# A four-layer graph network on one core: the launch's tests become a last sample of the schedule, the preparation moves among the first steps, and the order is searched anew

## The chip, the cores and the metric

The kernel runs on one core of one Trainium2 chip. A core has five engines, each with its own stream of instructions executed in order: TensorE (PE, with weight loads listed apart as PEld), VectorE (DVE), ScalarE (ACT), GpSimd (POOL) and SyncE (SP), which here only issues DMAs. The metric is the device time of one execution in microseconds (us), lower is better.

## The reference

The input `x` has 32 samples of 512 nodes with 256 features in float32, and one adjacency matrix of 512 by 512. Four layers follow one another, each with a normalisation ahead of it and its result added to `x`:

```python
h = jnp.maximum(_layernorm(x, axis=-1), 0.0); x = x + L0(h, adj, ...)  # 4-head attention, masked, output projection
h = jnp.maximum(_layernorm(x, axis=-1), 0.0); x = x + L1(h, adj, ...)  # MLP, graph attention (no mask), MLP, graph attention (mask)
h = jnp.maximum(_layernorm(x, axis=-1), 0.0); x = x + L2(h, adj, ...)  # 4-head graph attention, masked
h = jnp.maximum(_layernorm(x, axis=-1), 0.0); x = x + L3(h, adj, adj[None], ...)  # 8-head graph attention, mask and prior
```

In layer 0 `scores = q k^T / 8` where `adj != 0`, softmax, times `v`, times `wo`. In the graph attentions the score of nodes i and j is `leaky_relu(f1[i] + f2[j])`, followed by a softmax over j. Layer 3 adds `softplus(beta) * log(adj + 1e-6)` to the scores.

## The kernel before

Everything of the weights and masks stays in the on-chip memory; samples pass through one by one. A tile of nodes is 128 rows, so a sample is 4 such tiles (`NT`), and a 128 by 512 float32 square is one "block" (57 buffers) on chip or one "bank" (8) of the accumulator memory.

**Preparation** (lines 423 to 601, one block of code with an order written by hand). SP, ScalarE and GpSimd issue the loads of the adjacency (lines 430 and 431) and of all weights (432 to 463). VectorE casts the adjacency, TensorE transposes it (494 to 496), ScalarE copies it (500, 501). Masks are made from it: `mask0T` (546), `mask1` and `mask1T` (598 to 601, on GpSimd), and `mask3T`, which is the Relu, then Ln (510), then Exp scaled by `beta` (544). `projections` (483) multiplies the attention vectors of layers 2 and 3 into extra columns of `w2` and `w3`. The bias columns are turned by 12 small matmuls (566), the output bias `boa` and the column-sum correction `b2a` come from more matmuls (587 to 596).

**Tests.** Layers 0, 2 and 3 leave out the usual subtraction of a maximum in their softmax. Whether that is safe is tested on the weights: grams of `wq` and `wk` (517 to 535), row maxima of the adjacency (537), squares of the projected columns (553 to 559), and a short reduction (571 to 582), which ends in one integer, `go`. At the end of the kernel function all engines read `go` into a register (line 1367) and branch to `pipelined` (the quick form, taken with these inputs) or `general` (a safe loop).

**The schedule.** `pipelined` writes each sample's four layers as steps into a `Plan` (line 70), 32 samples in all. `Plan.order` (line 156) then decides the order in which all steps are emitted: a greedy simulation of the five engines with costs from `cost` (line 311). At each turn it takes the step that could start first; among equals the one with the smallest due time, `step.due = s * self.period - step.tail - step.urgent` (line 169), where `tail` is the longest chain behind the step and `urgent` comes from the table `URGENT` (line 47). `STARTS`, `PACE` and `LAYERS` (lines 44 and 45) say from when on a sample's layer may start; a step's sample may be at most `AHEAD = 3` samples ahead of the oldest one in flight. `issue` (line 265) emits the steps; the last 16 pieces of preparation, the list `late` (lines 619 and 620: products for `W_fc` and `W_hand`, and the final product for `mask3T`), are emitted one at every second step behind step 100. Since every recorded step is emitted by one line, nearly all instructions of the samples carry line 275 in the profile and are told apart by the names of their tiles: `h`, `pt`, `mm`, `sc`, `p`, `av`, `total`, `sm`.

Each layer opens with `norm_t` (line 648): statistics on VectorE, the inverse root `rs` on GpSimd, the scaled `h` on ScalarE, transposes `pt` on TensorE. Layer 0 (733) goes on with q, k and v, eight pairs of score matmuls `sc`, exponentials `p` on ScalarE, mask products and sums `total` on VectorE, and `av`. `normalise` (708) divides by the sums with the help of small DMAs. `separable` (902) serves layers 2 and 3; for the last samples it sums on TensorE (`direct`, 926).

Of the kernel before, what the change touches and what calls it, by code (L numbers as in the profile page):

```python
# [20 lines left out]
P = 128  # L21
# [21 lines left out]
PERIOD = 57.0  # L43
STARTS, PACE = (0.0, 11.0, 54.0, 70.0), 29.0
LAYERS = (0.0, 55.0, 178.0, 198.0)

URGENT = {
    "h:0": 49, "pt:0": 23, "mm:0": 7, "sc:0": 89, "p0:0": -655, "total:0": -158, "av:0": -3, "rc:0": -39,
    "oT:0": -103, "stats:1": 94, "h:1": 11, "pt:1": 6, "hT:1": 93, "mm:1": -5, "r1:1": -511, "total:1": -50,
    "rs1:1": -41, "av:1": -24, "o2:1": -243, "fb:1": -11, "s:1": 20, "r2:1": 94, "pt:2": 134, "mm:2": -7,  # L50
    "p3:2": -20, "av:2": -185, "total:2": -319, "sm:2": -35, "ue:2": -200, "stats:3": 6, "ms:3": -69,
    "h:3": -156, "hT:3": 112, "mm:3": -58, "e8:3": -19, "p3:3": -989, "av:3": -489, "total:3": -598,
    "raw:3": -11,
}
BLOCKS, KEEP = 57, 2
KEEP_BANKS = 0

LATE = 100
# [11 lines left out]
class Plan:  # L70
# [85 lines left out]
    def order(self):  # L156
# [16 lines left out]
        free = {tag: [0.0] * bufs for tag, (bufs, _) in self.tags.items()}  # L173
        held = {}
# [170 lines left out]
def gnn_stack_kernel(ctx: ExitStack, tc: tile.TileContext, a: dict, out: bass.AP):  # L345
# [21 lines left out]
    def load_rows(name, eng, cols):  # L367

        src = a[name]
        k = src.shape[0] // P  # L370
        t = const.tile([P, k, cols], F32, name=name)
        eng.dma_start(t[:, :, : src.shape[1]], T(src, "(k p) c -> p k c", p=P))
        return t
# [5 lines left out]

    def load_bcast(pool, name, eng, n):  # L380
        t = pool.tile([P, n], F32, name=name)
        load(t, name, eng)
        return t
# [30 lines left out]

# [5 lines left out]
    afc = first.tile([P, 2 * HID], F32, name="afc")  # L420
    ahd = first.tile([P, 2 * D], F32, name="ahd")
    prf = first.tile([P, HID], BF16, name="prf")
# [3 lines left out]
    with prep_stack, tc.manual_schedule():  # L426
# [5 lines left out]
        nc.scalar.dma_start(w2[:, :, H2 : H2 + D], T(a["L2_W"], "(k p) c -> p k c", p=P))  # L432
        src = a["L2_a"]
        a2 = prep.tile([P, 2, F2], F32, name="a2")
        nc.scalar.dma_start(a2, bass.AP(tensor=src.tensor, offset=src.offset, ap=[[0, P], [1, 2 * F2]]))
        for k in range(KD):
            nc.gpsimd.dma_start(
                T(w3[:, k, H3 : H3 + D], "p (h f) -> p h f", h=H3), T(a["L3_W"][:, k * P : (k + 1) * P, :], "h p f -> p h f")
            )
        bt = load_bcast(prep, "beta", nc.scalar, 1)  # L440
# [8 lines left out]
        wq = load_rows("wqT", nc.scalar, D)  # L449
        wk = load_rows("wkT", nc.sync, D)  # L450
        s3 = load_bcast(prep, "L3_a_src", nc.sync, D)
        d3 = load_bcast(prep, "L3_a_dst", nc.sync, D)
        m2 = load_rows("mlp2_w", nc.sync, D)
        wo = load_rows("woT", nc.sync, D)
        bo = load_bcast(prep, "bo", nc.sync, D)
        wv = load_rows("wvT", nc.sync, D)
        m1 = load_rows("mlp1_w", nc.sync, HID)
        wfc = load_rows("W_fc", nc.sync, HID + 2)
        f1a, r1a = wfc[:, :, HID : HID + 1], wfc[:, :, HID + 1 :]
        load(afc, "a_fc", nc.sync)  # L460
        wh = load_rows("W_hand", nc.sync, D + 2)
        load(ahd, "a_hand", nc.sync)
        w3o = load_rows("L3_WoT", nc.sync, D)

# [4 lines left out]
        one = prep.tile([P, 1], F32, name="one")  # L469
        nc.vector.memset(one, 1.0)  # L470
        H = H2 + H3
        tests = prep.tile([P, 2 * H + 5], F32, name="tests")
        nc.vector.memset(tests, 0.0)


        def project(w, kn, heads, f, vec, dst):

            for k in range(kn):
                pr = prep.tile([P, heads, f], F32, name="pr")
                nc.vector.tensor_tensor(pr, T(w(k), "p (h f) -> p h f", h=heads), vec, op=ALU.mult)  # L480
                nc.vector.tensor_reduce(dst(k), pr, axis=AX.X, op=ALU.add)

        def projections(w, h, f, vs, vd):
            project(lambda k: w[:, k, h : h + D], KD, h, f, vs, lambda k: w[:, k, :h])
            project(lambda k: w[:, k, h : h + D], KD, h, f, vd, lambda k: w[:, k, 3 * h + D :])
            nc.vector.tensor_scalar(w[:, :, h + D : 2 * h + D], w[:, :, :h], ALPHA - 1.0, None, op0=ALU.mult)
            nc.vector.tensor_scalar(w[:, :, 2 * h + D : 3 * h + D], w[:, :, 3 * h + D :], ALPHA, None, op0=ALU.mult)


        top = prep.tile([P, NT], F32, name="top")  # L490
# [6 lines left out]
        at = [prep.tile([P, N], F32, name="at", bufs=NT) for _ in range(NT)]  # L497
        m3 = [mask3T[:, j, :] for j in range(NT)]
        for j in range(NT):
            nc.scalar.copy(at[j], adjT[j])  # L500
            nc.scalar.activation(m3[j], adjT[j], AF.Relu)
        projections(w2, H2, F2, a2[:, 0:1, :].to_broadcast([P, H2, F2]), a2[:, 1:2, :].to_broadcast([P, H2, F2]))

        ab = prep.tile([P, 1], F32, name="ab")
        nc.vector.tensor_scalar(ab, bt, -1.0, None, op0=ALU.mult)
        nc.vector.tensor_tensor(ab, ab, bt, op=ALU.max)
        nc.scalar.activation(ab, ab, AF.Exp, scale=-1.0)
        nc.scalar.activation(ab, ab, AF.Ln, bias=one)
        for j in range(NT):
            nc.scalar.activation(m3[j], m3[j], AF.Ln, bias=eps)  # L510
        projections(w3, H3, F3, T(s3, "p (h f) -> p h f", h=H3), T(d3, "p (h f) -> p h f", h=H3))
        nc.vector.scalar_tensor_tensor(beta, bt, 0.0, ab, op0=ALU.max, op1=ALU.add)

        grams = []
        for w, name in ((wq, "bq"), (wk, "bk")):
            gp = pp.tile([64, N], F32, name="gp", bufs=2)
            for h in range(4):  # L520
                c = slice(h * 64, (h + 1) * 64)
                r = row[:, spans[name] + h * 64 : spans[name] + (h + 1) * 64]
                for k in range(KD):
                    nc.tensor.matmul(gp[:, c], w[:, k, c], w[:, k, c], start=(k == 0), stop=False)
                nc.tensor.matmul(gp[:, c], r, r, start=False, stop=True)
            gram = prep.tile([64, D], F32, name="gram", bufs=2)
            nc.vector.tensor_copy(gram, gp[:, :D])
            grams.append(gram)
        gp = pp.tile([64, N], F32, name="gp", bufs=2)
        for n in range(2):  # L530
            for h in range(4):
                c = slice(h * 64, (h + 1) * 64)
                nc.tensor.matmul(
                    gp[:, n * D + h * 64 : n * D + h * 64 + 64], grams[n][:, c], grams[1 - n][:, c], start=True, stop=True
                )
        for t in range(NT):
            nc.vector.tensor_reduce(top[:, t : t + 1], adjf[:, t, :], axis=AX.X, op=ALU.max)

        ok = prep.tile([P, NT], F32, name="ok")
        nc.vector.tensor_scalar(ok, top, 0.0, None, op0=ALU.is_gt)  # L540
        nc.vector.tensor_scalar(top, top, 0.0, None, op0=ALU.max)
        nc.scalar.activation(top, top, AF.Ln, bias=eps)
        for j in range(NT):
            nc.scalar.activation(m3[j], m3[j], AF.Exp, scale=beta)
        for j in range(NT):
            nc.vector.tensor_scalar(mask0T[:, j, :], at[j], 0.0, None, op0=ALU.not_equal)
        gab = prep.tile([64, D], F32, name="gab")
        nc.vector.tensor_copy(gab, gp[:, :D])
        nc.vector.tensor_tensor(gab, gab, gp[:, D:], op=ALU.mult)
        nc.vector.tensor_reduce(  # L550
            tests[:64, 2 * H + 1 : 2 * H + 5], T(gab, "p (h f) -> p h f", h=4), axis=AX.X, op=ALU.add
        )
        sq = prep.tile([P, KD, 2 * H], F32, name="sq")
        o = 0
        for w, h in ((w2, H2), (w3, H3)):
            for v in (w[:, :, :h], w[:, :, 3 * h + D :]):
                nc.vector.tensor_tensor(sq[:, :, o : o + h], v, v, op=ALU.mult)
                o += h
        nc.vector.tensor_tensor(tests[:, : 2 * H], sq[:, 0, :], sq[:, 1, :], op=ALU.add)
        bad = prep.tile([P, NT], F32, name="bad")  # L560
        nc.vector.tensor_scalar(bad, top, beta, SAFE_PRIOR, op0=ALU.mult, op1=ALU.is_le)
        nc.vector.tensor_tensor(bad, bad, ok, op=ALU.mult)
        nc.vector.tensor_reduce(tests[:, 2 * H : 2 * H + 1], bad, axis=AX.X, op=ALU.add)
        cp = pp.tile([P, N], F32, name="tp")
        for c in range(12):
# [446 lines left out]
    def general(stack):  # L1012

        for f in late:
            f()
# [409 lines left out]
```

## Time and profile before

| quantity | value |
|---|---|
| runs of the kernel, median (lowest to highest) | 4020.88 us (4020.18 to 4025.28), 3 runs |
| profiled execution, its own time | 4023.19 us |
| span of the profiled execution (first to last instruction) | 4021.3 us |
| TensorE, busy | 3933.0 us, 98% |
| VectorE, busy | 3303.2 us, 82% |
| ScalarE, busy | 2992.8 us, 74% |
| GpSimd, busy | 659.0 us, 16% |
| DMA | 274.80 MB, mean 68 GB/s |
| chain that ended last | 60% TensorE, 17% VectorE, 5% ScalarE, 4% DMA |

The profile is one execution recorded by the hardware. "Busy" is the time in which an engine had at least one instruction in work; matmuls overlap, so a busy TensorE is not one at its peak. A row of the timeline gives the start, the length, the engine, the line, the operation with its output and inputs, the shape and the count, and in brackets the idle time before it and what ended it. A row of the waits gives who waited, on whom, for how long in total, how often, and the longest. A float32 matmul appears as two instructions.

### The profile page before, as it was taken

The page shows a single profiled execution, that of the slowest core. Times are in us where ns is not written, and L with a number is a line of the kernel's source. Part 1 is how long each engine was busy: PE and PEld are TensorE (multiplying, and loading weights), DVE is VectorE, ACT ScalarE, POOL GpSimd, SP SyncE. Part 2 cuts the span into 40 slices and gives each one's busy share as a digit, 9 for nine tenths or more (in the row PEclk, how much of TensorE's full clock was granted, in tenths as well). Part 3 has the DMA queues.
Part 4 walks back from the last instruction along what each step waited for, and adds up shares of the span by engine and source line. Part 5 has one row for each costly group of instructions (what it writes and reads, how often), then busy time and mean ns, then how long its engine had stood idle before and what let it go on. Part 6 is the DMA issues. An engine that isn't in the chain of part 4 may idle for free.

```text
span 4021.3 us, 53382 instructions
## 1 busy us (share of the span) xinstructions
PE 3933.0 (98%) x17366; PEld 2179.0 (54%) x17366; DVE 3303.2 (82%) x6940; ACT 2992.8 (74%) x6386; POOL 659.0 (16%) x636
## 2 busy tenths in 40 slices
PE   8999999999999999999999999999999999999997
PEld 4655555555555655555555555655555555555553
DVE  6478888788888888888788887888888788887877
ACT  4568687877788777877877788777877777787766
POOL 2101110212121021110211211021110211111110
PEclk9999999999999999999999999999999999999998
DMA  2003231323332132322322323133322322322331
GB/s 81 17 17 90 64 85 54 80 64 69 75 80 72 46 90 63 74 70 67 86 64 61 82 65 87 47 71 73 83 69 67 85 64 59 78 70 71 65 79 49
DMA packets 198018, 274.80 MB, mean 68 GB/s; under 512 B 47273, under 2 KB 84394, under 8 KB 197730
## 3 DMA queue, kind: packets, MB, share of 16 engines
q1 hardware_dynamic: 144832, 176.05, 14.2%
q0 software_dynamic: 52064, 94.66, 13.8%
q8 instruction: 139, 2.28, 0.2%
q14 instruction: 149, 1.22, 0.1%
q10 hardware_dynamic: 834, 0.59, 0.1%
HBM read 157.74 MB, written 19.10 MB: 44 GB/s over the span
## 4 chain that ended last, share of the span: by engine, by line
PE 60%; DVE 17%; ACT 5%; DMA 4%; POOL 3%; issue 2%; SPq 0%; DVEq 0%; ACTq 0%; POOLq 0%
PE mm L275 30%; PE av L275 19%; PE pt L275 5%; DVE p L275 4%; PE sm L275 3%; PE sc L275 3%; DVE total L275 3%; ACT p L275 2%; POOL rs L275 2%; DVE x L275 2%; DVE stats L275 2%; DMA p<-p 2%; DVE ue L275 2%; DVE o L275 1%; DMA rc<-s 1%
## 5 line engine op out<-in xcount | busy, mean ns | idle before, releaser
L275 ACT ACTIVATE p<-R,e 128x512 f32<-128x512 f32 x1536 | 1005.4, 731 | 108.0 <-PE av L275 73.7
L275 DVE SCALAR_TENSOR_TENSOR p<-p,e,mask3T 128x512 f32<-128x512 f32 x1024 | 715.2, 741 | 179.5 <-ACT p L275 179.0
L275 PE MATMUL av<-p,v 128*128 128x512 f32 (+1 forms) x2048 | 700.5, 597 | 2.6 <-DVE p L275 2.5
L275 POOL TENSOR_TENSOR rs<-ve,mhalf 128x4 f32<-128x4 f32 x128 | 216.3, 1689 | 2214.4 <-DVE ve L275 1761.9
L275 DVE TENSOR_TENSOR total<-total,p 128x512 f32<-128x512 f32 x808 | 527.6, 683 | 0.8
L275 PE MATMUL av<-p,vs 128*32 128x512 f32 (+1 forms) x3072 | 491.0, 598 | 5.3 <-DVE p L275 5.3
L275 POOL DMA_DIRECT2D p<-p x360 | 323.0, 1095 | 1049.3 <-DVE p L275 412.9
L275 PE MATMUL mm<-W_fc,o 128*128 128x256 f32 (+1 forms) x2048 | 482.0, 381 | 4.9 <-ACT o L275 4.7
L275 PEld LDWEIGHTS av<-p,v 128*128 128x128 f32 (+1 forms) x2048 | 256.1, 163 | 348.5 <-issue 299.4
L275 PEld LDWEIGHTS mm<-W_fc,o 128*128 128x128 f32 x2048 | 375.4, 190 | 88.9 <-ACT o L275 22.3
L275 DVE TENSOR_TENSOR p<-p,mask0T 128x512 f32<-128x512 f32 x512 | 329.5, 680 | 65.0 <-ACT p L275 65.0
L275 DVE SCALAR_TENSOR_TENSOR p<-p,e,mask1T 128x512 f32<-128x512 f32 x512 | 355.0, 742 | 4.6 <-ACT p L275 4.3
L275 ACT ACTIVATE h<-x,ms,rs 128x256 f32<-128x256 f32 x512 | 276.8, 602 | 76.1 <-DVE ms L275 67.8
L275 PEld LDWEIGHTS av<-p,vs 128*32 128x32 f32 (+1 forms) x3072 | 133.1, 118 | 323.8 <-issue 238.2
L275 DVE TENSOR_TENSOR total<-p,p 128x512 f32<-128x512 f32 x404 | 279.7, 710 | 12.3 <-DMA p<-p 7.6
L275 ACT COPY v<-mm 128x256 f32<-128x256 f32 (+2 forms) x384 | 170.0, 452 | 138.7 <-PE mm L275 107.0
L275 ACT ACTIVATE p<-sc 128x512 f32<-128x512 f32 x512 | 256.1, 618 | 15.7 <-PE sc L275 15.5
L275 PE MATMUL mm<-w,hT 128*128 128x272 f32 (+1 forms) x1024 | 253.7, 395 | 8.0 <-ACT hT L275 8.0
L275 PE MATMUL mm<-hT,mlp_w 128*128 128x512 f32 x512 | 242.2, 600 | 2.4 <-ACT hT L275 1.5
L275 PE MATMUL sc<-qT,kT 64*128 64x512 f32 x1024 | 241.1, 606 | 0.2 <-ACT p L275 0.2
L275 PE MATMUL mm<-o,mlp_w 128*128 128x512 f32 x512 | 238.0, 594 | 0.0
L275 PE MATMUL av<-pT,v 128*128 128x512 f32 x512 | 226.6, 593 | 0.1
(189 smaller groups left out, 5977.3 us busy)
## 6 DMA issues: line engine op xcount, KB each, us to landing
R<-rd SPq DMA_DIRECT2D x384, 256.0 KB
p<-p POOLq DMA_DIRECT2D x360, 256.0 KB, 5.3
x<-in_x_dram SPq DMA_DIRECT2D x32, 512.0 KB
rc<-s SPq DMA_DIRECT2D x128, 128.0 KB
out_dram<-x SPq DMA_DIRECT2D x32, 512.0 KB
rc<-s SPq DMA_DIRECT2D x248, 64.0 KB
s<-sums SPq DMA_DIRECT2D x94, 8.0 KB
few<-s SPq DMA_DIRECT2D x94, 8.0 KB
```

What stands on the lines that cost most here:

```text
L275: getattr(getattr(self.nc, attribute), op)(*args, **kw)
```

## The change

- **Order.** `PERIOD`, `STARTS`, `PACE`, `LAYERS` and `URGENT` get new values; `BLOCKS` goes from 57 to 60. For the first 120 us of its simulation the plan regards 10 blocks as taken (`FILLED`), since the preparation now uses them.
- **Ahead of the samples** only the adjacency loads, `x` of sample 0, the loads of `wq`, `wk`, `wv` and of the bias rows, the casts and transposes of the adjacency, `mask1` (now on VectorE), `mask0T`, the Relu into `mask3T`, and the bias columns are left.
- **Among the first steps** a list of 36 pieces (`preparation`) is emitted, one at every odd step behind step 30, in its order: three groups of loads on SP, `mask1T` (now on VectorE, from `mask3T`), `boa`, the products of `W_fc`, the column sums, those of `W_hand`, the projections, `softplus` with the four Ln, and the four Exp with the last product of `mask3T`.
- **Tests** are recorded as steps of a 33rd sample, with the same matmuls; the adjacency is loaded and cast once more for the row maxima.
- **Branch.** `pipelined` runs without a condition; behind it `go` is read, and the general loop follows if it is below 1.
- **Layer 0** adds `boa` to `x` only behind the writes of `sm` (`q.behind(sm)`).

```diff
-PERIOD = 57.0
-STARTS, PACE = (0.0, 11.0, 54.0, 70.0), 29.0
-LAYERS = (0.0, 55.0, 178.0, 198.0)
+PERIOD = 100.0
+STARTS, PACE = (0.0, 4.0, 68.0, 98.0), 53.0
+LAYERS = (0.0, 1.0, 175.0, 132.0)
...
+    "pt:0": 66, "p0:0": -642, "total:0": 17, "av:0": -54, "pt:1": -26, "mm:1": -18, "total:1": -33,
+    "av:1": -24, "o2:1": -264, "s:1": -27, "stats:2": 8, "h:2": -90, "total:2": -351, "sm:2": -25,
+    "ue:2": -176, "mm:3": -112, "p3:3": -992, "av:3": -449, "total:3": -503, "sums:3": 18,
 }
-BLOCKS, KEEP = 57, 2
+BLOCKS, KEEP = 60, 2
...
-LATE = 100
+LATE = 30
+
+FILLED, FILLED_TO = 10, 120.0
...
+        free["block"][:FILLED] = [FILLED_TO] * FILLED
...
+        x0 = new_x()
+        nc.sync.dma_start(x0, xv[0])
+        wq = load_rows("wqT", nc.scalar, D)
...
         for t in range(NT):
             nc.vector.tensor_copy(adjf[:, t, :], adj[:, t, :])
             for j in range(NT):
                 nc.tensor.transpose(adjT[j][:, t * P : (t + 1) * P], adjf[:, t, j * P : (j + 1) * P], ident)
...
+            nc.vector.tensor_scalar(mask1[:, t, :], adjf[:, t, :], 0.0, -BIG, op0=ALU.is_le, op1=ALU.mult)
         for j in range(NT):
...
+            nc.scalar.activation(mask3T[:, j, :], adjT[j], AF.Relu)
+            nc.vector.tensor_scalar(mask0T[:, j, :], adjT[j], 0.0, None, op0=ALU.not_equal)
...
+    def preparation(block, bank):
...
+        def first_loads():
+            load_w(wo, "woT")
+            load(bo, "bo", nc.sync)
+            load_w(m1, "mlp1_w")
+            load_w(wfc, "W_fc")
...
+        def output_bias():
+            tp = bank("tp")
+            for k in range(KD):
+                nc.tensor.matmul(
+                    tp[:, :D], bvc[:, k : k + 1].to_broadcast([P, P]), wo[:, k, :], start=(k == 0), stop=(k == KD - 1)
+                )
+            nc.vector.tensor_tensor(boa, bo, tp[:, :D], op=ALU.add)
...
+        def softplus():
+
+            nc.vector.memset(one, 1.0)
+            nc.vector.tensor_scalar(ab, bt, -1.0, None, op0=ALU.mult)
+            nc.vector.tensor_tensor(ab, ab, bt, op=ALU.max)
+            nc.scalar.activation(ab, ab, AF.Exp, scale=-1.0)
+            nc.scalar.activation(ab, ab, AF.Ln, bias=one)
+            for j in range(NT):
+                nc.scalar.activation(mask3T[:, j, :], mask3T[:, j, :], AF.Ln, bias=eps)
+            nc.vector.scalar_tensor_tensor(beta, bt, 0.0, ab, op0=ALU.max, op1=ALU.add)
+
+        def mask_3(j):
+
+            nc.scalar.activation(mask3T[:, j, :], mask3T[:, j, :], AF.Exp, scale=beta)
+            nc.vector.tensor_tensor(mask3T[:, j, :], mask3T[:, j, :], mask1T[:, j, :], op=ALU.mult)
+
+        todo += [first_loads, second_loads, third_loads] + [partial(mask_t, j) for j in range(NT)] + [output_bias]
+        todo += [partial(fc, k, c) for k in range(KH) for c in range(2)] + [column_sums]
+        todo += [partial(hand, k, c) for k in range(KD) for c in range(2)]
...
+        return todo + [softplus] + [partial(mask_3, j) for j in range(NT)]
...
             for t in range(NT):
+                q.behind(sm)
                 q.gpsimd.tensor_tensor(xt[:, t, :], xt[:, t, :], boa, op=ALU.add)
...
+        def tests():
...
+            for t in range(NT):
+                ai, af = q.tile(big, [P, N], "ai", BLOCKS, keep=KEEP, tag="block", dtype=I32), block("af")
+                q.sync.dma_start(ai, a["adj"][t * P : (t + 1) * P, :])
+                q.vector.tensor_copy(af, ai)
+                q.vector.tensor_reduce(top[:, t : t + 1], af, axis=AX.X, op=ALU.max)
...
+                    for k in range(KD):
+                        q.tensor.matmul(gp[:64, c], w[:, k, c], w[:, k, c], start=(k == 0), stop=False)
+                    q.tensor.matmul(gp[:64, c], r, r, start=False, stop=True)
...
+            q.tensor.matmul(tp[:1, : 2 * H + 5], ones[:, 0:1], values, start=True, stop=True)
...
+            q.vector.tensor_copy(go, res[:, 5:6])
+
         for i in range(B):
             q.begin()
             q.left = B - i
...
+        q.begin()
+        q.layer = 3
+        tests()
+        late = preparation(
+            lambda n: big.tile([P, N], F32, tag="block", name=n, bufs=BLOCKS),
+            lambda n: psum.tile([P, N], F32, tag="bank", name=n, bufs=8),
+        )
         q.issue(tc, late)
...
+    with ExitStack() as stack:
+        pipelined(stack)
     fits = nc.values_load(go[0:1, 0:1])
-    with tc.If(fits > 0) as either:
-        with ExitStack() as stack:
-            pipelined(stack)
-    with either.Else():
+    with tc.If(fits < 1):
         with ExitStack() as stack:
             general(stack)
```

## The prediction

> **What bounds the kernel now.** I read the page's busy times first, then the busy time of the engines in stretches of the span, then the instructions in order of time for the first 40 us, then what TensorE waits for in the last 200 us, and last the distance between output stores in the middle. From the page:
>
> ```profile
> PE 3933.0 (98%) x17366; PEld 2179.0 (54%) x17366; DVE 3303.2 (82%) x6940; ACT 2992.8 (74%) x6386; POOL 659.0 (16%) x636
> ```
>
> TensorE is in use 98% of a span of 4021.3 us; 88 us of it are idle. Where they lie is in the stretches (length; then busy time of TensorE, its weight loads, VectorE, ScalarE and GpSimd, each with its count; clock; DMA):
>
> ```profile
> 0.00:40.00 40.00, 25.71 (x128) 21.33 (x128) 22.56 (x82) 14.81 (x25) 20.20 (x22) 1.00 0.59 189
> 40.00:200.00 160.00, 155.96 (x589) 85.97 (x589) 92.68 (x211) 86.33 (x172) 18.96 (x21) 1.00 0.05 14
> 200.00:400.00 200.00, 195.82 (x813) 108.48 (x811) 153.33 (x331) 149.91 (x330) 19.00 (x18) 1.00 0.21 54
> 400.00:3700.00 3300.00, 3270.22 (x14528) 1814.14 (x14528) 2785.46 (x5827) 2523.08 (x5407) 570.95 (x545) 1.00 0.30 71
> 3700.00:3850.00 150.00, 147.92 (x641) 85.12 (x642) 130.29 (x266) 111.64 (x237) 15.99 (x16) 1.00 0.23 54
> 3850.00:4022.00 172.00, 137.39 (x671) 63.99 (x669) 118.86 (x225) 107.00 (x219) 13.90 (x15) 0.88 0.26 66
> ```
>
> Idle is 14.3 us before 40, 4.0 to 200, 4.2 to 400, 29.8 in the 3300 us of the middle, 2.1, and 34.6 in the last 172. But the first 25.7 "busy" us are preparation, not samples, so the lead is worth nearly all of its 40 us. Its order of time (start, length, engine, line, operation, operands):
>
> ```profile
> 11.15 0.43 DVE L494 CAST adjf<-adj 128x512 f32<-128x512 int32 x1 [2.97 <-DMA adj<-in_adj_dram]
> 23.32 5.27 PE L566 MATMUL tp<-ones,row 1*128 1x1 f32 x24
> 29.91 0.14 DVE L582 CAST go<-res 1x1 int32<-1x1 f32 x1
> 30.72 0.92 SPq L275 DMA_DIRECT2D x<-in_x_dram  x2
> 34.36 0.42 DVE L595 TENSOR_TENSOR boa<-bo,gp 128x256 f32<-128x256 f32 x1 [4.31 <-PE gp L592]
> 35.39 1.41 DVE L275 BATCH_NORM_STATS2 stats<-x 128x6 f32<-128x256 f32 x4 [0.55 <-DVE b2a L596]
> 39.52 2.16 PE L275 MATMUL pt<-ident,h 128*128 128x128 f32 x8 [5.20 <-ACT h L275]
> ```
>
> The last adjacency rows are cast at 11.15; the tests run to 29.91 (`go`); only behind the branch does SP ask for x, at 30.72; VectorE works on `boa`, `b2a` until 34.85 and starts sample 0 at 35.39; TensorE's first sample matmul is at 39.52. At the other end TensorE waits (waiter, releaser, us, times, longest):
>
> ```profile
> PE mm L275 <- DVE oT L275: 9.8, 2, 8.6
> PE av L275 <- DVE p L275: 5.3, 2, 3.7
> PE mm L275 <- DVE rc L275: 5.2, 1, 5.2
> ```
>
> Those are dependences of the last samples: nothing else is left to run. In the middle two stores of the output four samples apart give the pace:
>
> ```profile
> 1409.33 0.40 SPq L275 DMA_DIRECT2D out_dram<-x  x1
> 1895.20 0.40 SPq L275 DMA_DIRECT2D out_dram<-x  x1
> ```
>
> 485.9 / 4 = 121.5 us a sample; the next four take 484.6, 121.1. Idle there is about 0.9 us a sample, so only the order of TensorE's own work could change it much.
>
> **What the Trainium skill says.** "Perfetto Trace Analysis", Identifying the Most-Contended Engine: busy time of matmuls does not tell how near TensorE is to its limit. That agrees: 98% busy holds cold and mode-switching stretches. "TensorE: Matmul & The Clock Gate", The HAM clock gate: after idling, TensorE runs at half clock for some 3.4 us. The trace agrees: from 42.16 to 46.37 the 128x512 matmuls follow each other by 0.85 us, then by 0.43. Both kernels idle a few us ahead of sample 0, so both pay. "ScalarE: Activation LUTs", What ACT_TABLE_LOAD costs: 1283 ns, with a drain 2.66 us. The trace shows 1.28 us, and the next activation begins 1.29 us after the load did (16.58, 17.87), so no drain is seen and I use 1.28.
>
> **The change, part by part.**
>
> *Lead.* Gone from ahead of sample 0: the tests (grams, row maxima, `top`, `sq`, `res`), Ln and Exp of `mask3T`, both projections, `boa`, `b2a`, the branch, and 16 of the early loads (`L2_W`, `L3_W`, `W_fc`, both `mlp` weights and others). Left: four adjacency loads, casts, transposes, masks, the bias columns. x of sample 0 moves to the fifth place on SP, ahead of wk and wv. SP's four adjacency issues end at 4.98, so x is asked for at about 5 and, taking the longest landing seen (30.72 to 35.39, 4.7 us), is there by 10. The chain then is: last adjacency cast (11.15 now; with far less in front of it I take 9, bounds 7.5, the second row's 2.5 us after issue, and 11.15), cast 0.43 and its transposes 1.12, then the 24 bias-column matmuls 5.27, copy and scaling on VectorE 0.34, together 16.2; bn_stats to first transpose 39.52 - 35.39 = 4.1; TensorE starts at 20.3 instead of 39.5. The four `mask1` move from GpSimd (8.0 us) to VectorE at some 0.36 each (`mask0T`: 1.43 for four); they lie beside the waits for adjacency and the bias columns, and would cost 1.4 without them. **-19 us**, bounds -17 and -20.7.
>
> *Moved among the first steps.* TensorE takes `boa` (2.08) and the column sums (3.41) inside the schedule: 5.5 at the lead's duration, perhaps 2.7 warm: **+4.5**. The weight loads (some 4 MB) are still issued by SP early, because SP only waits for destinations: 17 issues of 0.45 us from about 8 us on; now the same loads landed in the 20 us in which DMA moved 209 and 359 GB/s. I cost them at nothing as W_fc is read no sooner than 20; if one is late TensorE stands at the column sums, or VectorE at `fc`, for the missing us. VectorE takes over eight projections (0.42 + 0.42 each, 6.7), four `mask1T` (1.4), `boa` and small ones, some 10 us, beside the 10 us of `fc`, `hand` and `mask_3` that already sit among the steps. Their cover is sample 0 and 1's q, k, v on TensorE, when VectorE is at 1.1 and 2.7 of 10 us now (40 to 60). ScalarE gets two table loads, four Ln (2.54) and four Exp (2.56), small ones: 8.1 us in its queue ahead of attention exponentials; behind those wait VectorE's mask products and then TensorE's `av`. From 60 to 100 VectorE is at 9.9 to 10 of 10 now, so a hold-up there is not made good. Bounds 0 and 8: **+3**. GpSimd's additions of `boa` go behind `sm`; 4 x 0.73 us, under the division's DMA trip: nothing.
>
> *Tests.* TensorE's part cost 3.8 + 2.8 + 2.8 + 2.0 + 0.3 = 11.7; VectorE's about 8, ScalarE two table loads, SP six loads. As sample 32 they may start only when sample 28 has left its buffers, at about 3819 (its store), and then lie in a stretch with 36 us of idle TensorE and 53 of idle VectorE: bounds 0 and 11.7, **+3**. The value of `go` is read behind everything: 0.47 to 0.55 us on each engine now, plus a branch that a similar branch at the end replaces: bounds 0 and 3, **+1**.
>
> Sum: -19 + 4.5 + 3 + 3 + 1 = -7.5.
>
> *New order.* Not to be read off the old trace; bounded by it. It may win back a part of the last 172 us and of the filling stretch (34.6 + 8.2 idle), and has three more blocks (60 for 57); a pace of 1 us a sample either way is 30 us. Ends -40 and +35. I take a fifth of those 43 us: **-8**.
>
> -15.5 on a span of 4021.3 is 4005.8; the profiled execution took 4023.2, 1.9 more than its span, and the median of the runs is 4020.9, so in the median's terms **4005**.
>
> **Rivals.**
> A. Forecast: lead gained, small costs, order as good or a bit better: 3990 to 4012. Speaks for it: TensorE has no other work in the first 40 us, and the loss afterwards is slight.
> B. The order also gives 1 us a sample or most of the tail: 3970 to 3990. For it: 0.9 us idle and some us of mode switching a sample; against: no view says that this was left over by oversight.
> C. The lead is gained but the hold-up moves: ScalarE's 8.1 us and VectorE's 20 us of preparation fall into the attention of samples 0 and 1, where VectorE is full, and TensorE stands for 8 to 12 more, as `av` waits on `p`: 4013 to 4029, centre 4020.
> D. The other side: the middle's pace. A new order that switches TensorE's mode more often costs the same each sample; from (7.5 + 8) / 30 = 0.5 us a sample (121.2 to 121.7) the kernel is slower; at 1 us, 4021 - 7.5 + 30 = 4043. For it: the whole order changed; against: nothing in the middle is touched otherwise.
>
> **How the numbers follow.** A 0.54, B 0.14, C 0.19, D 0.13. No change is within 0.2%, 8 us, which is about what a measurement of this kernel tells. Faster: A + B = 0.68; same: C, 0.18 of its 0.19; slower: D and the rest, 0.14. The range 3977 to 4031 leaves out the lower part of B and most of D.
>
> **What would show it.** Right: the first h transpose at 19 to 23 us, x asked for at 5; `boa` after the first transposes; idle TensorE between 20 and 80 under 10 us; test matmuls after 3800; stores 121 us apart. Wrong: ScalarE's Ln or table loads as releaser of TensorE's waits (C); stores over 121.7 apart (D) or under 120.5 (B); test steps at the end of the chain that ended last.

## The result, and the profile after

The changed kernel takes 4085.4 us (median of 4, 4082.32 to 4091.51) against 4023.1 us for the kernel before on the same chip: a ratio of 1.0157, 95% interval 1.0139 to 1.0174. It is slower by about 62 us, where 4005 was forecast. The profiled execution took 4087.0, its span 4085.0 (before: 4023.2 and 4021.3).

The page's busy times of the kernel after:

```profile
PE 3979.4 (97%) x17366; PEld 2188.0 (54%) x17366; DVE 3352.1 (82%) x6952; ACT 2963.1 (73%) x6384; POOL 625.5 (15%) x626
```

TensorE has the same 17,366 matmuls and is busy 46 us longer for them. So most of the loss is not counted as idle. The stretches (length; busy time and count of TensorE, weight loads, VectorE, ScalarE, GpSimd; clock; DMA):

```profile
0.00:40.00 40.00, 28.26 (x122) 18.43 (x124) 20.00 (x66) 15.16 (x27) 9.43 (x16) 0.83 0.62 189
40.00:200.00 160.00, 139.92 (x526) 79.17 (x523) 80.93 (x191) 77.92 (x159) 6.79 (x8) 0.94 0.04 14
200.00:400.00 200.00, 192.35 (x814) 103.25 (x813) 166.73 (x340) 141.90 (x315) 28.32 (x26) 0.97 0.19 45
400.00:3700.00 3300.00, 3272.45 (x14292) 1801.94 (x14291) 2783.81 (x5740) 2460.82 (x5315) 539.81 (x534) 1.00 0.29 70
3700.00:3850.00 150.00, 149.24 (x666) 81.75 (x665) 129.33 (x272) 110.08 (x245) 25.81 (x26) 1.00 0.27 68
3850.00:4086.00 236.00, 197.18 (x956) 103.41 (x954) 171.33 (x347) 157.26 (x328) 15.30 (x16) 0.93 0.23 64
```

Two things stand out. From 40 to 200 TensorE is idle for 20 us, where the kernel before was idle for 4, and its granted clock is 0.94 there, where it was 1.00. And in the 3300 us of the middle it is busy for 2 us more than before, but with 14,292 matmuls where there were 14,528: 1.6% fewer for the same busy time. The count shows what the busy time hides. The beginning in order of time:

```profile
2.62 0.43 SPq L423 DMA_DIRECT2D x<-in_x_dram  x1
7.33 0.43 DVE L442 CAST adjf<-adj 128x512 f32<-128x512 int32 x1 [0.27 <-DMA adj<-in_adj_dram]
8.54 2.83 PE L451 MATMUL tp<-ones,row 1*128 1x1 f32 x24
17.83 2.16 PE L275 MATMUL pt<-ident,h 128*128 128x128 f32 x8 [6.46 <-ACT h L275]
30.84 0.42 DVE L511 TENSOR_TENSOR boa<-bo,tp 128x256 f32<-128x256 f32 x1 [10.71 <-PE tp L508]
51.44 0.20 ACT L552 ACTIVATE ab<-ab 128x1 f32<-128x1 f32 x1 [9.20 <-DVE ab L551]
51.66 1.28 ACT L553 ACT_TABLE_LOAD   x1
53.15 2.54 ACT L555 ACTIVATE mask3T<-mask3T,eps 128x512 f32<-128x512 f32 x4
57.66 6.90 PE L275 MATMUL av<-p,v 128*64 128x512 f32 x16 [13.46 <-ACT p L275]
```

The first transposes of sample 0 come at 17.83, 21.7 us sooner. But then VectorE stands for 10.7 us at `boa`, the first of its pieces that needs TensorE (the four `mask1T` are done by 20), because TensorE does q and k of sample 0 ahead of the matmuls for it. VectorE's further pieces therefore run from 31 to 51; ScalarE stands for 9.2 us at the start of `softplus`, which waits for VectorE's `ab`; behind that stand the exponentials of layer 0, and behind those TensorE, for 13.5 us.

The waits of TensorE in the last 200 us, and the stores:

```profile
PE pt L275 <- ACT p L275: 6.8, 1, 6.8
PE mm L275 <- DVE rc L275: 5.2, 1, 5.2
PE mm L275 <- DVE oT L275: 3.9, 1, 3.9
```

```profile
1394.11 0.40 SPq L275 DMA_DIRECT2D out_dram<-x  x1
1889.61 0.40 SPq L275 DMA_DIRECT2D out_dram<-x  x1
```

The end waits for much the same as before. The pace, the distance of the output stores for one sample, is 495.5 / 4 = 123.9 us a sample (121.5 before); over the 16 samples from the 9th to the 25th store 123.6, before 121.2.

**Where the 64 us of span went.** Since busy time hides waits, I counted the work: each matmul instruction at the distance at which such instructions follow one another at full clock in these traces (0.427 us for 512 columns on the whole array; a float32 matmul is two of them), times its share of the array where groups of 32 or 64 columns, or of 64 rows, run beside each other. Both kernels come to 3711.9 us for the samples. The rest of each stretch is lost to TensorE (us). The last two columns are experiments told of below:

| stretch | before | after | after, R dearer | before, R dearer |
|---|---|---|---|---|
| 0 to 400 | 67.2 | 75.8 | 64.3 | 62.5 |
| 400 to 1400 | 56.2 | 61.0 | 47.5 | 47.4 |
| 1400 to 2400 | 46.4 | 65.1 | 49.4 | 42.6 |
| 2400 to 3400 | 45.2 | 63.7 | 49.7 | 45.3 |
| 3400 to 3900 | 36.2 | 37.4 | 41.7 | 41.8 |
| 3900 to the end | 58.1 | 70.2 | 63.9 | 48.9 |

Of 64 us, 9 are lost in the first 400, 42 in the next 3000 and 12 at the end. In the middle the loss is inside the groups of 32-column matmuls: the sum of (distance to the next start, less the time it should be) went from -1.1 to +1.4 us a sample there. Changes of TensorE's mode (whole array, groups of 32 columns, of 64 columns, of 64 rows) fell from 17.5 to 16.0 a sample.

Which wait stands behind it? Two groups of the page, of before and then of after (busy, mean ns | idle time ahead of them and what ended most of it):

```profile
L275 ACT ACTIVATE p<-R,e 128x512 f32<-128x512 f32 x1536 | 1005.4, 731 | 108.0 <-PE av L275 73.7
L275 PE MATMUL av<-p,vs 128*32 128x512 f32 (+1 forms) x3072 | 491.0, 598 | 5.3 <-DVE p L275 5.3
```

```profile
L275 ACT ACTIVATE p<-R,e 128x512 f32<-128x512 f32 x1536 | 1001.9, 731 | 183.6 <-DMA R<-rd 180.1
L275 PE MATMUL av<-p,vs 128*32 128x512 f32 (+1 forms) x3072 | 539.6, 598 | 14.4 <-DVE p L275 13.8
```

The same 3,072 matmuls (2,048 of 32 columns, 1,024 of 64) show 48.6 us more busy time; experiment 9 will show that this rise is not the loss itself. And ScalarE now waits for the DMA of `R` (the rows of scores that `separable` writes to DRAM as `rd` and reads back, spread over all partitions): 180 us where it had 16.5, as the waits of before say:

```profile
ACT p L275 <- DMA R<-rd: 16.5, 9, 6.2
```

### The profile page after: what moved, and what is told of

Same layout as the page of the kernel before. It is cut to its first block, busy times and chain, and to the rows that moved or that the text cites. A ratio compares the mean times of both kernels' runs of the same rounds, so it can differ in the third digit from the quotient of the medians.

```text
span 4085.0 us, 53285 instructions
## 1 busy us (share of the span) xinstructions
PE 3979.4 (97%) x17366; PEld 2188.0 (54%) x17366; DVE 3352.1 (82%) x6952; ACT 2963.1 (73%) x6384; POOL 625.5 (15%) x626
## 3 DMA queue, kind: packets, MB, share of 16 engines
q1 hardware_dynamic: 148196, 177.69, 13.5%
## 4 chain that ended last, share of the span: by engine, by line
PE 55%; DVE 25%; ACT 11%; DMA 4%; issue 2%; POOL 2%; SPq 1%; DVEq 0%; POOLq 0%; ACTq 0%
PE mm L275 27%; PE av L275 20%; DVE p L275 11%; ACT p L275 6%; DVE total L275 5%; PE pt L275 4%; PE sm L275 3%; DMA R<-rd 3%; DVE x L275 2%; DVE stats L275 2%; ACT e L275 2%; POOL rs L275 2%; DVE ue L275 1%; SPq L275 1%; DVE oT L275 1%
## 5 line engine op out<-in xcount | busy, mean ns | idle before, releaser
L275 DVE SCALAR_TENSOR_TENSOR p<-p,e,mask3T 128x512 f32<-128x512 f32 x1024 | 749.9, 776 | 155.9 <-ACT p L275 155.9
L275 PE MATMUL av<-p,v 128*128 128x512 f32 (+1 forms) x2048 | 697.1, 600 | 13.5 <-ACT p L275 13.5
L275 POOL TENSOR_TENSOR rs<-ve,mhalf 128x4 f32<-128x4 f32 x128 | 191.8, 1501 | 2973.3 <-DVE ve L275 2863.6
L275 PE MATMUL av<-p,vs 128*32 128x512 f32 (+1 forms) x3072 | 539.6, 598 | 14.4 <-DVE p L275 13.8
L275 PE MATMUL mm<-W_fc,o 128*128 128x256 f32 (+1 forms) x2048 | 473.8, 380 | 0.0
L275 PEld LDWEIGHTS av<-p,vs 128*32 128x32 f32 (+1 forms) x3072 | 143.9, 118 | 348.5 <-issue 203.8
L275 DVE TENSOR_TENSOR total<-p,p 128x512 f32<-128x512 f32 x404 | 267.1, 683 | 0.3 <-PE mm L275 0.3
L275 PE MATMUL mm<-hT,mlp_w 128*128 128x512 f32 x512 | 233.9, 598 | 1.0 <-ACT hT L275 0.6
L275 PE MATMUL sc<-qT,kT 64*128 64x512 f32 x1024 | 231.7, 598 | 0.0
L275 PE MATMUL mm<-o,mlp_w 128*128 128x512 f32 x512 | 226.0, 593 | 0.4 <-DVE o L275 0.4
L275 PEld LDWEIGHTS mm<-w,hT 128*128 128x128 f32 x1024 | 190.3, 191 | 60.3 <-ACT p L275 21.5
```

The source lines that it names most:

```text
L275: getattr(getattr(self.nc, attribute), op)(*args, **kw)
```

## The experiments

Times are medians; "before" was 4021.0 to 4022.4 us beside them. The changed kernel's 4085.4 was taken beside 4023.1, so a difference to it is uncertain by about 2 us for that alone. "Moves" are the parts of the change other than the order.

**1 and 2. The two halves.** One kernel has all the moves with exactly the order of before (the tests emitted one by one near the end), the other the preparation, tests and branch of before with the new order.

```diff
 # all moves, old order
+        tests = self.samples.pop()
+                if n >= TESTS_AT and n % 3 and tests:
+                    self.emit(tests.pop(0))
-                q.behind(sm)
 # nothing moved, new order
+                if step.sample == last:
+                    continue
```

> All moves of the change (short lead, preparation among the first steps, tests late in the schedule, branch behind) with exactly the order of steps of the kernel before: its parameters and 57 planned blocks, the additions of boa again behind h, held only until boa is there; the tests are emitted one by one among the last 400 steps. Theory 'order' (the new order costs 2.4 us a sample): stores 121.2 us apart in the middle, total 4003 to 4025, the lower end if the lead's 20 us are kept, the upper if the preparation eats them. Rival 'moves' (what was moved slows every sample): stores near 123.6 apart, total 4070 to 4090.

> The other half: preparation, tests and branch ahead of the samples as in the kernel before, but the steps in exactly the order of the changed kernel, additions of boa behind sm included; the a vectors of W_fc and W_hand are loaded into blocks behind the branch to make room for 60 blocks. Theory 'order': stores 123.6 us apart, total 4080 to 4100. Rival 'moves': 121.2 apart, total 4018 to 4030.

Measured: 4037.7 (1.0043, 1.0026 to 1.0059) with the old order, pace 120.8; 4082.6 (1.0155, 1.0138 to 1.0172) with the new one, pace 123.4. The order alone costs 61.6 us. The moves cost 16.7 with the old order; with the new one only 2.8 remain, which is within the intervals (some 7 us either way). With the old order the pace is even 0.4 us a sample better than before; why was not tried (that kernel has 60 blocks where its plan counts 57).

**3. GpSimd's additions.** In the new order some additions of `boa` run beside VectorE's products with `mask3T`. Of the 1,024 products 32 lie beside an addition; these take 1.81 us in the mean (not 1.07, as the expectation says), the others 0.74. Here the additions go behind `sm` for the first two samples only.

```diff
+                if len(q.samples) < 3:
-                q.behind(sm)
+                    q.behind(sm)
```

> The changed kernel with the additions of boa on GpSimd behind sm only for the first two samples; from the third on they may run as early as before. The order of the steps on TensorE, VectorE, ScalarE and SyncE stays the same. Theory 'collision' (the additions hold VectorE's products with mask3T, which take 1.07 us beside them and 0.74 otherwise, one in eight samples' worth 3.4 us, and TensorE's av waits): products near 0.74, 1 to 1.9 us less a sample, total 4032 to 4058. Rival 'too tight an order' (the av and sm groups come too early for VectorE in any case): under 0.4 us less a sample, total 4074 to 4088.

Measured: 4089.3 (1.0170, 1.0153 to 1.0187), pace 123.5. The mean of all products falls from 0.776 to 0.751 us, and the time does not. The collision is real and costs nothing that counts.

**4. The hold-up.** The last 15 pieces of preparation (projections, `softplus`, the Exp of `mask3T`) from step 240 on, one at every sixth step.

```diff
-                    assert step.layer == 0
-                    if n % 2:
+                    assert step.layer < 2
+                    if n % 2 if len(late) > 15 else n > 240 and not n % 6:
```

> The changed kernel with the last 15 pieces of the preparation (projections of layers 2 and 3, softplus with Ln, the products of mask3T) emitted from step 240 on, one every 6 steps, instead of at steps 73 to 101. Theory 'hold-up' (TensorE's 13.5 us wait at 44 to 58 is ScalarE standing before softplus, which waits for VectorE's projections, and the cold clock after it costs 4 more): the wait goes, total 12 to 20 us less, 4065 to 4073. Rival 'VectorE bound' (VectorE has the same work to do and the wait turns up later): under 5 us less, 4080 to 4088.

Measured: 4063.9 (1.0111, 1.0094 to 1.0127), 21.5 us less than the changed kernel. By the count of losses some 14 us of it lie in the first 400 us, about the wait of 13.5; the rest is spread over the later stretches and was not traced. The waits of TensorE in its first 110 us no longer have the 13.5:

```profile
PE pt L275 <- ACT h L275: 7.7, 2, 6.5
PE adjT L444 <- DVE adjf L442: 5.1, 2, 4.7
PE mm L275 <- DVE oT L275: 4.6, 1, 4.6
```

Pace 123.3 (123.6): the middle is nearly untouched by it.

**5 and 6. R from elsewhere.** To take `R`'s dependence on `rd` away, all its loads read one row of `x`, in the changed kernel and in the one before.

```diff
+                    if op == "dma_start" and args and self.kinds.get(args[0].tensor.name) == "R":
+                        args = (args[0], bass.AP(tensor=self.x.tensor, offset=self.x.offset, ap=[[0, P], [1, N]]))
```

> The changed kernel with its order, but each load of R (the row of source scores, sent through DRAM in layers 2 and 3) reads a fixed row of x in place of the row that has just been stored, so it need not wait for that store; the scores of layers 2 and 3 are therefore other numbers. Theory 'R late' (ScalarE waits 6.6 us a sample for R in the middle of the changed kernel, none before, and VectorE's products and TensorE's groups of av then come late): ScalarE's waits for R go, stores 121.8 us or less apart, total 4025 to 4050. Rival 'VectorE late' (the groups come too early for VectorE by its own work): less than 0.6 us a sample gained, total 4070 to 4088.

> The same edit in the kernel before, R from a fixed row of x. Both theories: no wait for R stands there, so stores 121.0 to 121.4 us apart, total within 8 us of 4021; under 4010 would say that R's trip costs this order too.

Measured: 4247.8 (1.0562) and 4138.3 (1.0290). The edit failed its purpose: with every load of `R` on the same 2 KB of DRAM, the median time of a 2 KB packet went from 84 to 116 ns in the kernel before, and ScalarE waited 160 and 67 us for `R`. It says only that a slower `R` is dear in both orders.

**7 and 8. VectorE's load.** The second and third additions into `total` of layer 3 left out (4.9 us of VectorE a sample).

```diff
+                if step.layer == 3 and step.calls[0][2] and self.kinds.get(step.calls[0][2][0].tensor.name) == "total" and step.calls[0][0] == "vector":
+                    if step.calls[0][2][1].tensor.name == step.calls[0][2][0].tensor.name:
+                        continue
```

> The changed kernel with its order, without the second and third of the additions on VectorE into each total of layer 3 (8 of 0.61 us a sample, 4.9 us), so the softmax sums of four heads lack two terms. Theory 'VectorE late': the waits inside the groups of 32-column av and sm go, stores 121.8 us or less apart, total 4025 to 4050. Rival 'R late': the groups still wait for products that wait for ScalarE, under 1.0 us a sample gained, 4055 to 4088.

> The same additions left out of the kernel before. Both theories: TensorE sets this order's pace and VectorE has room, so stores 120.6 to 121.3 us apart and total 4005 to 4022; a gain as large as in the changed kernel would say that VectorE's work costs both orders alike and explains no difference.

Measured: 4084.6 (1.0146, 1.0123 to 1.0168), pace 123.5; and 4016.1 (0.9985) in the kernel before. These additions of VectorE, at least, are not what is late in the new order.

**9 and 10. R loaded, but not read.** The exponentials of layers 2 and 3 read a mask that has long been there; the loads of `R` and every engine's order stay.

```diff
+                    if op == "activation" and self.kinds.get(args[1].tensor.name) == "R":
+                        args = (args[0], self.mask) + tuple(args[2:])
```

> The changed kernel, where ScalarE's 1,536 exponentials of the lower two layers read a mask that has long been there in place of the loaded row R; R is still loaded, the order of every engine is untouched, and the output isn't the reference's (exp of a mask value stands in for exp of R). Theory that the new order leaves R too little time to arrive: ScalarE's 106 us of waits for R in the middle go, the 32-column groups no longer come late, the pace falls from 123.6 to about 121 us a sample and the time from 4085 to about 4045 or below. Rival, that the late groups come of the order in which VectorE and ScalarE work and R's wait only fills time that they would lose anyway: pace stays at 123 or more, 4075 to 4090.

> The same edit in the kernel before (the output isn't the reference's either). It showed no wait of ScalarE for R in the middle, so both theories expect no change: 4015 to 4026. If it too gets faster by 15 us or more, the edit removes something else than the waits for R, and the run beside it says less.

Measured: 4026.4 (1.0016, 1.0010 to 1.0023), pace 121.7, the excess in the 32-column groups down from 1.4 to 0.3 us a sample (-1.1 in the kernel before); and 4011.6 (0.9975) before. Without the wait 59 us go in the changed kernel, 10 in the other. SyncE still issues `R` as late as in the changed kernel (3.4 us behind `rd` in the median in both), and the exponentials last 731 ns in both: what went is the wait itself. So the wait for `R` is what the new order pays for. The busy time of the 3,072 matmuls is not its measure, as it hardly fell from 539.6:

```profile
L277 PE MATMUL av<-p,vs 128*32 128x512 f32 (+1 forms) x3072 | 530.9, 597 | 10.1 <-DVE p L277 9.3
```

Nor is every wait for `R` a loss. Experiment 1, at a pace of 120.8, has more of them than the kernel before, many of about 3 us:

```profile
ACT p L299 <- DMA R<-rd: 56.9, 25, 5.8
```

How the wait comes about in the new order, at one of its places (SyncE, then ScalarE):

```profile
1428.66 0.63 SPq L275 DMA_DIRECT2D rd<-rT  x1
1433.89 4.64 SPq L275 DMA_DIRECT2D R<-rd  x4
1439.63 0.72 ACT L275 ACTIVATE p<-R,e 128x512 f32<-128x512 f32 x1 [9.88 <-DMA R<-rd]
```

From the issue of `rd` to the first use of `R` it is 11.0 us. Between 400 and 3900 ScalarE waited over 1.5 us for `R` 24 times, behind 19 writes of `rd`; from each of these to the first use it is 10.7 in the median (8.3 to 11.2). The planner counts, by line 341 of the kernel, 0.4 us for the issue and then 3.4 us plus the bytes over 190e3 for each transfer: 3.84 for `rd`, 5.18 for `R` of 256 KB, and 0.05 after each, 9.1 together. It thus put the exponentials some 1.6 us too early there, in an engine that works in order, and what stands behind them is late too. The long waits themselves are mostly planned: here ScalarE has nothing left at 1429.75, 1.1 us after the issue of `rd`, so by the planner's own price 8 of its 9.9 us were foreseen. How 19 times some 1.6 us, about 30, grow into the 59 was not followed.

The traces also say where the planner's price is short. From the issue of `rd` to that of `R`, which waits for `rd` to land, it counts 3.9 us. In the changed kernel, 22 of the 57 writes of `rd` between 400 and 3900 moved their first packet over 1.6 us after the issue, and all 22 stood among some 250 packets of GpSimd's own transfers `p<-p` (issued to add exponentials up); there `R` came 4.6 us after `rd` in the median. The 30 writes without such packets all moved sooner, with `R` 2.0 us behind in the median; five more had such packets near and were not late. In the kernel before, one write of 57 stood among such packets. The 24 waits over 1.5 us all stand behind writes of those 22. That the new order put `rd` behind these transfers is read from the traces; no run took the transfers away.

**11, 12 and 16. What the moves can bring with the old order.** The tests of experiment 1 spread (loads 500 steps earlier, the operations one to every two to six steps); then also the 15 late pieces from step 240; then those from step 504, one at every twelfth.

```diff
+            at[22000 + 6 * n if n < grams else 22118 + 3 * (n - grams) if n < sums else 22360 + 2 * (n - sums)] = t
-                    if n % 2:
+                    if n % 2 if len(late) > 15 else n > 240 and not n % 6:   # or n > 500 and not n % 12
```

> All moves of the change with the order of the kernel before (as in the first experiment, 4037.7), but the tests' loads issued some 500 steps earlier and the tests' operations one to every two to six steps in place of one a step. If the tail of the first experiment (694 us from the 25th store to the end, 668.5 before) came of the crowded tests: about 680 in the tail and 4020 to 4028 in all. If the tests cost that much wherever they stand: 4034 to 4040.

> The kernel of the run beside it (moves of the change, order of before, tests spread), and the last 15 pieces of the preparation put off to steps 240 and later, one to every six steps, as in the fourth experiment. Theory (the lead's gain of about 20 us is real, and only the hold-up of 21.5 us eats it): some 18 to 21 us less than the run beside it, about 4000 to 4007, and faster than both kernels. Rival (with the order of before the hold-up is refilled later): within 6 us of the run beside it.

> The kernel of the twelfth run (moves of the change, order of before, tests spread: 4021.7), whose late pieces stood between steps 240 and 330 and there made TensorE stand for 8 us at 103 to 113 us. Here they come between steps 504 and 672, one to every 12 steps. If the place of the pieces alone decides what is kept of the lead: 5 to 10 us less, 4012 to 4017. If what is gained at the start is lost anyway before the first store: 4019 to 4024.

Measured: 4025.9 (1.0013), 4021.7 (1.0003, 0.9995 to 1.0011), 4026.2 (1.0016, 1.0007 to 1.0024). The place of the tests was worth 12 us, as thought. The late pieces were worth 4 or nothing: the rivals were right. TensorE's work done on the samples by a given time, counted as above (us), shows why:

| done by | before | after | exp. 11 | exp. 12 | exp. 16 | exp. 4 |
|---|---|---|---|---|---|---|
| 40 us | 0.2 | 14.9 | 11.2 | 11.2 | 11.4 | 11.7 |
| 100 us | 49.5 | 49.5 | 50.7 | 61.1 | 64.0 | 59.8 |
| 150 us | 95.8 | 95.5 | 97.5 | 99.7 | 113.3 | 108.7 |
| 200 us | 144.4 | 144.7 | 146.4 | 148.5 | 148.1 | 158.2 |

Put off, the pieces take their toll where they then stand: between 100 and 150 in experiment 12, between 150 and 200 in experiment 16, whose TensorE here waits for `o` on ScalarE, held by 5.5 us of table loads and Ln:

```profile
180.46 2.54 ACT L586 ACTIVATE mask3T<-mask3T,eps 128x512 f32<-128x512 f32 x4
185.75 6.46 PE L306 MATMUL mm<-W_fc,o 128*128 128x258 f32 x19 [5.49 <-ACT o L306]
```

**13, 14 and 18. The order searched again with R dearer, and the control.** In the changed kernel the tables of the order were searched anew, with `R`'s price in the planner 1.5 us higher (13), the same with the late pieces put off (14), and with the price as it was (18).

```diff
-    return 0.4, 3.4 + size / 190e3
+    return 0.4, 3.4 + size / 190e3 + (1.5 if out.tensor.name.startswith("R") else 0.0)   # control: 0.0
```

> The changed kernel with an order searched again, in which the planner's table gives R's transfer 1.5 us more than before (all else in the kernel as in the changed one, tests and branch among it). Theory that the new order's loss is R coming later than planned for: ScalarE's waits for R fall well below 180 us, the pace comes to 120 to 122 us a sample, and the time to about 4015 to 4045 (4026 where R wasn't read). Rival, that an order from this table is slow on the chip for another reason (any searched order packs something too tightly): pace 123 or more and 4065 or above.

> The kernel of the run beside it, with the last 15 pieces of the preparation from step 240 on, one to every six steps. If the start's gain of some 20 us can be kept: 15 to 22 us less than the run beside it, about 4000 to 4025. If the pieces stop ScalarE again a little later, as with the order of before: within 6 us of it.

> The control to the run with R dearer (4031.6): the changed kernel with an order searched again for as long and in the same way, but with R's price in the planner's table as it was. Theory (the price of R decides, not the luck of a new search): ScalarE again waits more than 100 us for R, and the time is 4050 or above. Rival (any further search would have found a better order): no large waits for R, and 4020 to 4040.

Measured: 4031.6 (1.0026, 1.0015 to 1.0036), 4026.4 (1.0013, 1.0006 to 1.0020) and 4101.2 (1.0195, 1.0179 to 1.0210). ScalarE's waits for `R` in the first and the last (waiter, releaser, us, times, longest):

```profile
ACT p L273 <- DMA R<-rd: 10.5, 7, 6.0
```

```profile
ACT p L273 <- DMA R<-rd: 198.0, 81, 10.0
```

The control waits for `R` like the changed kernel; with R dearer the waits are nearly gone and 54 of the 62 us with them. The 1.5 us added bring the planner's 9.1 to 10.6, about what was measured. The late pieces gave 5 us, the rival's value, as with the old order. One order was tried of each kind here, and the order of before also came from the cheap price and hardly waits (16.5 us), so the price doesn't force a bad order; it fails to keep the search from one.

**15. Without the tests.** Their steps keep their places in the plan, but are not issued; `go` is set by a copy.

```diff
+                if step.sample == len(self.samples) - 1:
+                    if step.calls[0][2][0].tensor.name == self.go.tensor.name:
+                        self.nc.vector.tensor_copy(self.go, self.ones[:1, 0:1])
+                    continue
```

> The changed kernel without Launch's tests: the planned order keeps their places, but nothing of them is issued, and the flag is set by one small copy from a constant, so the branch stays and is always taken to the fast path; the output is the same, the inputs aren't tested. If the tests cost what the prediction priced (about 3 us): 4080 to 4084. If they hold up the tail of the last samples, whose 708 us were 39 more than before: 4070 or less. The order's part in the tail is what remains.

Measured: 4073.1 (1.0137, 1.0120 to 1.0153). The tests at the end cost 12.3 us by the medians, 8 by the two ratios, and the four runs lie 13 us apart: some 8 to 12. Neither forecast of the expectation holds, it lies between. The tail from the 25th store to the last is 697.4 without them, 708.0 with, 668.5 before, and 697.8 in experiment 13. So some 29 us of the longer tail belong to the new orders themselves. That is not all loss: in experiment 13 the 25th store came 22 us sooner than before. The table of losses, not the tail, says what is lost there.

**17. A faster kernel.** The kernel before, with nothing moved, and an order searched with `R`'s price 2 us higher.

```diff
+    return 0.4, 3.4 + size / 190e3 + (2.0 if out.tensor.name.startswith("R") else 0.0)
```

> The kernel before, all of it (its preparation, its tests at the start, its branch), with an order searched with R's transfer 2 us dearer in the planner's table. Not reading R made the kernel before 10 us faster, so its order too has some loss at R. Theory: 4005 to 4018, faster than both kernels, and no wait of ScalarE for R of more than 20 us in all. Rival (a searched order gains in one place and loses in another): 4019 or above, its pace above 121.5 us a sample.

Measured: 4000.9 (0.9949, 0.9935 to 0.9962), faster than both kernels; pace 120.9. Its page and its wait for `R`:

```profile
PE 3924.6 (98%) x17366; PEld 2187.6 (55%) x17366; DVE 3321.9 (83%) x6940; ACT 3000.8 (75%) x6386; POOL 631.5 (16%) x636
```

```profile
ACT p L270 <- DMA R<-rd: 6.3, 2, 6.1
```

By the table of losses it gains on before 4.7 us in the first 400, 8.8 to 1400, 3.7 to 3400, and 9.2 behind 3900, and loses 5.6 between. Experiment 10 bounds what `R` can have given at some 10 us; the rest is what any new search may find, and was not taken apart.

## Why the prediction was wrong

- **New order, -8: this step failed.** Experiment 2 measured +61.6, outside its ends of -40 and +35. The ends were too narrow: I priced the pace at 1 us a sample either way, and it moved by 2.4. The sentence behind rival D, that nothing in the middle is touched otherwise, was the error: an order sets how much time each DMA round trip has before an in-order engine asks for its result, so every transfer was touched. The sum has no term for `R`: it put these trips at nothing without a word, and experiment 9 shows that in the new order the waits for them cost 59 us. That the trace before shows only 16.5 us of such waits was a property of that order.
- **Rival D** had the right side and place, and its threshold of 0.5 us a sample was passed by far (2.4). Its mechanism was wrong: mode changes became fewer. At 0.13 it was too small.
- **What would show it:** TensorE's idle time in the middle, from which the prediction argued, could not have shown it (29.8 us before, 27.6 after). The stores 123.9 apart did, as named for D, and the count of matmuls for the same busy time. Idle TensorE between 20 and 80 was to stay under 10 us; it was 14.0.
- **Lead, -19:** right, a little small. The first transposes came 21.7 us sooner, beyond the bound of 20.7, since the 24 bias-column matmuls took 2.83 us, not 5.27, and the last cast came at 7.33.
- **Moved matmuls, +4.5:** 1.03 for `boa` and 1.85 for the column sums, 2.9. The weight loads, put at nothing, held none of TensorE's waits of the first 110 us.
- **Hold-up, +3 (0 to 8): failed by size.** Experiment 4 gives 21.5 for it in the new order, some 14 of them in the first 400 us. The cover named, TensorE's q and k of sample 0, was not used: `boa` stood ahead of all but the masks among VectorE's pieces and waited for a matmul behind that very work, so VectorE stood through its cover and ScalarE after it. The prediction counted busy time and not who stands first in the queue. Rival C named the mechanism, but as an alternative to A; it was there at any rate, and TensorE's wait of 13.5 was longer than its 8 to 12. How much of the lead is kept is a matter of the whole start: with the old order and with the dearer R, putting the pieces off brought 4, 0 and 5 us. Before, that work lay in a stretch in which TensorE had nothing to do; among the samples no place was found where it was free.
- **Tests, +3 (0 to 11.7):** some 8 to 12 in experiment 15, near the upper bound: the idle time of the tail covers little of them.
- **`go`, +1:** not measured by itself.

The parts that were moved sum to some 3 us in the new order, within the noise (4082.6 in experiment 2 against 4085.4): the lead, the hold-up and the tests cancel. That they cancel so nearly is luck, as two of the terms were far off. The result is the order.

## What to carry to other kernels

Where a planner fixes the order of in-order engines, a round trip priced some 1.6 us short at the wrong places can cost more than moving a whole preparation gains; before trusting a searched order, compare the planner's price of each round trip with the distance from issue to use where the trace shows a wait, price it on the long side, and look at what else the DMA engines carry then. Moving work out of an idle lead is worth the lead only if the place it goes to is free in every queue it enters, and the first piece in each queue decides. And a busy share says nothing on lateness inside groups of matmuls: compare counts for equal busy time.

## What the runs showed of the hardware

- A short wait inside a stream of matmuls is booked as busy: from 400 to 3700 us TensorE shows 3272 us busy with 14,292 matmuls and 3270 with 14,528.
- Loads of `R` that all spread the same 2 KB row of DRAM were slow: 116 against 84 ns for a packet in the median, and 116 us more in the kernel before.
- A GpSimd addition of 128x256 beside a VectorE product of 128x512 lengthened the product from 0.74 to 1.81 us in the mean (32 products), 3.38 at worst.
- A small write that stood among some 250 packets of GpSimd's transfers took longer to be seen: the load that waits for it was issued 4.6 us after it in the median (22 writes, 3.5 to 5.2), and 2.0 where none stood there (30 writes).
